# A block-diagonal 128x128 product in a state space layer, written as two products of its 64x64 blocks

## The chip, the cores and the metric

The kernel runs on one core of one Trainium2 chip. The metric is the device time of one execution in microseconds (us). It is given as the median of several executions, beside one execution that the hardware profiler recorded.

## The reference, cut to what matters

The reference is a decoder of four layers over 32 sequences of 64 tokens (2,048 tokens, 256 wide), all in 32-bit floats. Two of its twelve sublayers, `L1_attn` (32 heads) and `L2_attn` (8 heads), are state space mixers. Each head keeps a state that decays by a factor per token:

```python
dt = jax.nn.softplus(dt + dt_bias)
A = -jnp.exp(A_log)
dA = jnp.exp(dt * A)

def step(h, inp):
    dA_t, dt_t, x_t, B_t, C_t = inp
    u = (dt_t[:, :, None] * x_t)[..., None] * B_t[:, :, None, :]
    h = dA_t[:, :, None, None] * h + u
    y = jnp.einsum('bhpn,bhn->bhp', h, C_t)
    return (h, y)
...
y = jnp.moveaxis(ys, 0, 1) + D_param[None, None, :, None] * xs
g = y * _silu(gate)
g = g * jax.lax.rsqrt(jnp.mean(g * g, axis=-1, keepdims=True) + EPS) * norm_w
return jnp.einsum('bli,di->bld', g, W_out)
```

A sequence has 64 tokens and begins with a zero state. So the output of token i is a sum over the tokens s up to i, and the weight of s holds exp of the sum of `dt * A` over the tokens after s up to i. This weight is called the decay here. The kernel makes all decays of a sequence and a head at once, as a 64x64 matrix.

## The kernel before

**Tokens and tiles.** The 2,048 tokens are 16 tiles of 128 partitions, two sequences of 64 in each tile. The state space layers take two tiles at a time (index `t`). `unit_ssm` (L1197) normalises, projects and makes `dt`, `da` (which is `dt * A`) and the masked product of B and C, `cb`. `unit_ssm_heads` (L1229) then does eight heads at a time: four calls for a pair of tiles in `L1_attn`, one call in `L2_attn`. With eight pairs of tiles in each layer that is 32 + 8 = 40 calls.

**The decays.** In each call `ra` (2 tiles, 8 heads, 64 columns) holds `da` of token s in row s, and zero in the columns of earlier tokens. The constant `after` (L53) is 1 where the row is a later token than the column *and both belong to the same sequence*: a 128x128 matrix of two 64x64 blocks on the diagonal and zeros elsewhere. The product of `after` with `ra[:, t]` (L1249, through the helper `prod`, L755) is the sum of `da` over the tokens between, for 8 heads x 64 columns = 512 columns, in one PSUM bank. ScalarE takes `Exp` of it into `m` (L1250), VectorE multiplies by `cb` (L1251), and the 64x64 products of L1273 use it. There are two such products in a call, 80 in the kernel.

**PSUM and TensorE.** Every product writes a tile `mm` of one bank, of which there are eight. A product of 128 rows by 128 columns of weights takes the whole array. One with 64 rows and 64 columns takes a quarter, chosen by the partitions that it reads and writes. Such quarters are used elsewhere already: L1273 (64 columns), and `cross_out` (L1015), where a 64x64 block of the context meets 512 columns. There, and at L1273, the two row halves write into different banks; the two column halves of one row half share a bank.

**The order.** Nothing runs in the order of the Python code. A `Recorder` (L376) collects every operation with its dependencies, and `Order.run` (L562) then places them one after the other: of the operations that are ready, the one that can start first on its engine, by the planner's own durations. Some operations may go to either of two engines (`either`, `combine`), and the planner chooses. The streams of three groups of tiles (8, 6 and 2) are woven together, and a limit (`horizon`, 120 us of TensorE work by the same durations) keeps the planner from running too far ahead. All instructions are issued from one line, L2326, so groups of the profile are told apart by the names of tiles. The durations of TensorE come from these lines:

```python
part = (32 if k <= 32 else 64 if k <= 64 else 128) * (32 if m <= 32 else 64 if m <= 64 else 128) / 16384

if part == 1:
    return max(n, m) * 0.00168 + 0.004
return max(0.068, n * 0.00168 * part * 1.2 + 0.02)
```

For a full product over 512 columns they give 0.864 us, and for a 64x64 one over 512 columns 0.278 us.

In the names of the profile, `pair_mm` are the projections of the state space layers (128 rows, 256 columns), `ssm_heads_mm` all products of `unit_ssm_heads`, and `ssm_heads_mm<-ssm_heads_b,__init___consts` of the shape 128x512 the product with `after`.

Of the kernel before, what the change touches and what calls it, by code (L numbers as in the profile page):

```python
# [199 lines left out]
def bc(ap, axis, n):  # L200

    u = ap.unsqueeze(axis)
    s = list(u.shape)
    s[axis] = n
    return u.broadcast_to(s)
# [11 lines left out]
def split(ap, a, pat="p (a b) -> p a b"):  # L217
    return ap.rearrange(pat, a=a)
# [425 lines left out]
class Net:  # L644
# [584 lines left out]
    def unit_ssm_heads(self, W, nh, g, j, st):  # L1229

        nc = self.nc
        nx = nh // 2
        wx, wg, wr, wo, par = W
        cw = par["cw"].rearrange("p (c k) -> p c k", k=4)
        upto = self.k("upto")
        first, last = j == 0, j + 4 == nx
        hT, dt, da, cb = st["hT"], st["dt"], st["da"], st["cb"]

        ra = self.b4(2, 8, 64)
        nc.combine(  # L1240
            ra, bc(da[:, :, 2 * j : 2 * j + 8], 3, 64), bc(bc(upto, 1, 2), 2, 8), ALU.mult
        )
        xs = self.b4(4, GT)
        for u in range(0, 4, 2):
            self.conv(par, cw, xs[:, u : u + 2, :], self.pair(wx, (j + u) * P, hT), j + u)
        gs, m = self.b4(4, GT), self.b4(2, 8, 64)
        for t in range(2):
            ps = self.mm()
            self.prod(ps, [(self.k("after"), ra[:, t])])  # L1249
            nc.scalar.activation(m[:, t], split(ps, 8), AF.Exp)  # L1250
        nc.vector.tensor_tensor(m, m, bc(cb, 2, 8), ALU.mult)  # L1251
        for u in range(0, 4, 2):
            nc.scalar.activation(gs[:, u : u + 2, :], self.pair(wg, (j + u) * P, hT), AF.Silu)
        xd = self.b4(2, 8, 64)
        for t in range(2):
            ps = split(self.mm(), 4)
            for u in range(4):
                self.transpose(ps[:, u, :], xs[:, u, t * P : (t + 1) * P])
            nc.vector.tensor_tensor(
                xd[:, t],  # L1260
                ps.rearrange("p c (h n) -> p (c h) n", h=2),
                bc(dt[:, t, 2 * j : 2 * j + 8], 2, 64),
                ALU.mult,
            )

        y = self.b4(4, GT)
        pv = [self.mm().rearrange("p (u t n) -> p u t n", u=4, t=2) for b in range(2)]
        for t in range(2):
            for u in range(4):
                for b in range(2):  # L1270
                    rb = slice(64 * b, 64 * b + 64)
                    for h in range(2):
                        nc.tensor.matmul(  # L1273
                            pv[b][64 * h : 64 * h + 64, u, t],
                            xd[rb, t, 2 * u + h, :],
                            m[rb, t, 2 * u + h, :],
                            start=True,
                            stop=True,
                        )
        y5 = y.rearrange("p u (t b n) -> p u t b n", t=2, b=2)  # L1280
        x5 = xs.rearrange("p u (t b n) -> p u t b n", t=2, b=2)
        for b in range(2):
            for u in range(4):
                nc.vector.scalar_tensor_tensor(
                    y5[:, u, :, b], x5[:, u, :, b], par["d"][:, j + u : j + u + 1], pv[b][:, u], ALU.mult, ALU.add
                )
        nc.combine(y, y, gs, ALU.mult)
        sq = self.b4(4, GT)
        nc.scalar.activation(sq, y, AF.Square)


        if first:
            st["acc"] = [self.mm() for _ in range(2)]
        acc = st["acc"]
        pq = acc[0][:, 256:]
        for u in range(4):
            if u == 3:
                for v in range(4):
                    rows = slice(32 * v, 32 * v + 32)
                    nc.tensor.matmul(pq[rows, :], self.k("unit"), sq[:, v, :], start=False, stop=False)  # L1300
            for t in range(2):
                nc.tensor.matmul(
                    acc[t][:, :256],
                    y[:, u, t * P : (t + 1) * P],
                    wo[(j + u) // 8][:, (j + u) % 8, :],
                    start=(first and u == 0),
                    stop=(last and u == 3),
                )
        if not last:
            return  # L1310

        sums = self.tmp(GT)
        self.evac(sums, pq)
        pr = self.mm()
        for t in range(2):
            self.prod(pr[:, t : t + 1], [(sums[:, t * P : (t + 1) * P], self.k("ones")[:, 0:1])])
        ve, rs = self.sm(2), self.sm(2)
        nc.vector.tensor_scalar(ve, pr[:, :2], 1.0 / (nx * P), 1e-5, ALU.mult, ALU.add)
        self.power(rs, ve)
        for t in range(2):  # L1320
            self.outproj(2 * g + t, acc[t][:, :256], rs[:, t : t + 1])
# [1103 lines left out]
```

## Time and profile before

| | |
|---|---|
| median of 9 executions | 3210.51 us (3189.45 to 3213.98) |
| the profiled execution | 3188.77 us |
| its span, first to last instruction | 3186.7 us |
| TensorE (PE) busy | 2978.2 us, 93% of the span |
| VectorE (DVE) busy | 2216.9 us, 70% |
| ScalarE (ACT) and GpSimd (POOL) busy | 1413.5 us and 1412.6 us, 44% each |
| mean granted TensorE clock | 0.969 |

The page gives the busy time of each engine, and groups instructions by tile names and shape. A 32-bit matmul leaves two records in the trace, so the 80 products with `after` are 160 records. The duration of one record includes the time in which the next record already streams. How long a matmul holds TensorE is therefore read from the distance between the starts of two records, not from a duration. "PEld" is the weight load, which runs beside the matmul before it.

### The profile page before, as it was taken

What the parts mean: (1) busy time and instruction counts of PE and PEld (TensorE: products, weight loads), DVE (VectorE), ACT (ScalarE), POOL (GpSimd) and SP (SyncE); (2) the same over time, 40 slices, a digit from 0 to 9 for tenths busy, and PEclk for the clock granted to TensorE, in tenths of its full rate; (3) what the DMA queues carried; (4) which work ended last, traced back from release to release, by engine and by line L of the source; (5) the groups of instructions that cost most, each with busy time, mean ns of one, the idle gap of its engine ahead of it and who ended that gap; (6) DMA issues with size and microseconds to landing.
All of it is one profiled execution on the core that took longest, in us unless ns stands there. A gap on an engine that the chain in (4) does not pass through costs nothing.

```text
span 3186.7 us, 66434 instructions
## 1 busy us (share of the span) xinstructions
PE 2978.2 (93%) x26862; PEld 2369.1 (74%) x26862; DVE 2216.9 (70%) x5239; ACT 1413.5 (44%) x2623; POOL 1412.6 (44%) x1278
## 2 busy tenths in 40 slices
PE   8999999999999899999989999999999988996689
PEld 7888887777777788788767777767787757774467
DVE  5564347775456577755889988777657879786684
ACT  1233325566442233544545555553335654453341
POOL 4442232224454555225653456565634655354230
PEclk9999999999999999999999999999999999997789
DMA  4104120031431533012001010103561120224240
GB/s 154 33 16 171 62 87 10 1 144 57 178 132 43 154 118 117 30 57 70 28 26 31 1 64 8 69 19 125 171 241 62 61 69 15 82 92 142 82 178 27
DMA packets 112949, 256.97 MB, mean 81 GB/s; under 512 B 26309, under 2 KB 73688, under 8 KB 100228
## 3 DMA queue, kind: packets, MB, share of 16 engines
q1 hardware_dynamic: 97860, 204.73, 18.5%
q0 software_dynamic: 14784, 48.01, 4.4%
q8 instruction: 212, 3.47, 0.4%
q14 instruction: 93, 0.76, 0.1%
HBM read 177.34 MB, written 78.77 MB: 80 GB/s over the span
## 4 chain that ended last, share of the span: by engine, by line
PE 65%; DVE 20%; ACT 5%; POOL 5%; issue 3%; DMA 1%; SPq 0%; DVEq 0%; POOLq 0%; ACTq 0%
PE L_xattn_mm L2326 9%; PE L_attn_mm L2326 8%; PE cross_out_mm L2326 8%; PE ssm_heads_mm L2326 7%; PE pair_mm L2326 5%; DVE ssm_heads_b L2326 4%; PE L_ffn_mm L2326 4%; PE turn_mm L2326 4%; PE rope_mm L2326 3%; PE L_block_mm L2326 3%; DVE L_xattn_b L2326 2%; PE L_dense_mm L2326 2%; PE L_experts_mm L2326 2%; PE heads_mm L2326 1%; DVE L_xattn_sm L2326 1%
## 5 line engine op out<-in xcount | busy, mean ns | idle before, releaser
L2326 PE MATMUL pair_mm<-norm_b,load_ssm_w 128*128 128x256 f32 x1280 | 306.9, 385 | 0.9 <-DVE ssm_heads_b L2326 0.6
L2326 PEld LDWEIGHTS pair_mm<-norm_b,load_ssm_w 128*128 128x128 f32 x1280 | 238.4, 192 | 45.5 <-issue 9.1
L2326 DVE SCALAR_TENSOR_TENSOR ssm_heads_b<-pair_mm,load_ssm_wp,ssm_heads_b 128x252 f32<-128x252 f32 (+2 forms) x480 | 218.9, 473 | 17.9 <-ACT ssm_heads_b L2326 8.0
L2326 POOL TENSOR_TENSOR L_xattn_sm<-L_xattn_sm,__init___consts 128x8 f32<-128x8 f32 (+2 forms) x62 | 178.5, 2881 | 86.1 <-DVE L_xattn_sm L2326 77.3
L2326 ACT ACT_TABLE_LOAD x153 | 196.3, 1283 | 32.8 <-PE L_block_mm L2326 11.6
L2326 POOL TENSOR_TENSOR norm_sm<-norm_sm,__init___consts 128x1 f32<-128x1 f32 (+1 forms) x142 | 88.6, 626 | 257.4 <-DVE norm_sm L2326 246.0
L2326 ACT COPY L_xattn_b<-L_xattn_mm 128x512 f32<-128x512 f32 x189 | 110.8, 588 | 188.8 <-PE L_xattn_mm L2326 188.6
L2326 ACT COPY turn_b<-turn_mm 128x512 f32<-128x512 f32 x202 | 112.7, 588 | 179.7 <-PE turn_mm L2326 176.5
L2326 PE MATMUL ssm_heads_mm<-load_ssm_w,ssm_heads_b 128*128 128x256 f32 x640 | 161.2, 396 | 6.7 <-issue 3.7
L2326 PE MATMUL rope_mm<-norm_b,load_L_attn_w 128*128 128x128 f32 x1280 | 160.9, 282 | 3.8 <-DMA load_L_attn_w<-in_a_wk 3.2
L2326 PEld LDWEIGHTS rope_mm<-norm_b,load_L_attn_w 128*128 128x128 f32 x1280 | 152.8, 196 | 9.0 <-issue 6.0
L2326 POOL TENSOR_TENSOR ssm_heads_b<-ssm_heads_b,ssm_heads_b 128x1024 f32<-128x1024 f32 x30 | 70.8, 2360 | 188.6 <-DVE ssm_heads_b L2326 142.5
L2326 PEld LDWEIGHTS ssm_heads_mm<-load_ssm_w,ssm_heads_b 128*128 128x128 f32 x640 | 119.3, 194 | 42.2 <-issue 19.8
L2326 PEld LDWEIGHTS L_xattn_mm<-norm_b,load_L_xattn_w 128*128 128x128 f32 x1024 | 119.3, 192 | 8.3 <-issue 7.0
L2326 ACT ACTIVATE ssm_heads_b<-pair_mm,load_ssm_wp 128x256 f32<-128x256 f32 x160 | 81.6, 560 | 96.8 <-PE pair_mm L2326 94.9
L2326 PE MATMUL L_xattn_mm<-norm_b,units_L_xattn_w 128*128 128x128 f32 x1024 | 122.5, 276 | 2.1 <-ACT norm_b L2326 1.4
L2326 PE MATMUL L_xattn_mm<-norm_b,load_L_xattn_w 128*128 128x128 f32 x1024 | 123.1, 276 | 0.0
L2326 POOL DMA_INDIRECT slots<-norm_b,L_ffn_sm x84 | 91.0, 1083 | 69.4 <-DVE L_ffn_b L2326 22.9
L2326 PEld LDWEIGHTS L_xattn_mm<-norm_b,units_L_xattn_w 128*128 128x128 f32 x1024 | 118.3, 192 | 4.3 <-ACT norm_b L2326 1.8
L2326 DVE TENSOR_TENSOR rope_b<-rope_mm,__init___consts 128x512 f32<-128x512 f32 x160 | 102.7, 680 | 25.3 <-PE rope_mm L2326 14.4
L2326 PE MATMUL L_attn_mm<-load_L_attn_w,L_attn_b 128*128 128x256 f32 x512 | 119.2, 385 | 0.7 <-ACT L_attn_b L2326 0.5
L2326 PE MATMUL cross_out_mm<-units_L_xattn_w,cross_out_b 128*128 128x256 f32 x512 | 116.1, 383 | 3.9 <-ACT cross_out_b L2326 3.9
(437 smaller groups left out, 7740.8 us busy)
## 6 DMA issues: line engine op xcount, KB each, us to landing
queue<-far_w SPq DMA_DIRECT2D x14, 1024.0 KB
L_block_w<-in_f_rows SPq DMA_DIRECT2D x16, 770.0 KB
load_ssm_w<-in_s_in SPq DMA_DIRECT2D x12, 1024.0 KB
parts<-far_w SPq DMA_DIRECT2D x10, 1024.0 KB
slots<-far_w SPq DMA_DIRECT2D x16, 548.0 KB
L_experts_b<-slots SPq DMA_DIRECT2D x32, 274.0 KB
units_L_xattn_w<-kept_x SPq DMA_DIRECT2D x8, 1024.0 KB
L_parts_b<-parts SPq DMA_DIRECT2D x14, 512.0 KB
```

The source lines that it names most:

```text
L2326: done = getattr(getattr(nc, e), method)(*map(real, op.args), **{k: real(v) for k, v in op.kw.items()})
```

## The change

The product over 128 rows becomes two products over 64 rows each, with the two diagonal blocks of the same constant. The first reads partitions 0 to 63 and writes partitions 0 to 63 of the bank, the second does the same with 64 to 127. The blocks left out hold zeros only. `Exp` and everything behind it stay as they are.

```diff
         for t in range(2):
+
             ps = self.mm()
-            self.prod(ps, [(self.k("after"), ra[:, t])])
+            for b in range(2):
+                rb = slice(64 * b, 64 * b + 64)
+                nc.tensor.matmul(ps[rb], self.k("after")[rb, rb], ra[rb, t], start=True, stop=True)
             nc.scalar.activation(m[:, t], split(ps, 8), AF.Exp)
```

The planner reads the new shapes, so its durations for these operations change with them: 0.864 us for the old product, 2 x 0.278 = 0.556 us for the two new ones. The order of the instructions is planned anew from that.

## The prediction

> **What bounds the kernel now.** I read the page's busy times first, then the chain that ended last, then busy times by stretch, and last the order of TensorE's records around a product with `after`.
>
> ```profile
> PE 2978.2 (93%) x26862; PEld 2369.1 (74%) x26862; DVE 2216.9 (70%) x5239; ACT 1413.5 (44%) x2623; POOL 1412.6 (44%) x1278
> PE 65%; DVE 20%; ACT 5%; POOL 5%; issue 3%; DMA 1%; SPq 0%; DVEq 0%; POOLq 0%; ACTq 0%
> ```
>
> The first line is the busy time of the engines, the second the chain's shares by engine. TensorE is busy 93% of the span and carries 65% of the chain: it is the bound, with 3186.7 - 2978.2 = 208.5 us in which it is idle. In the busy times by stretch (us, then PE, PEld, DVE, ACT and POOL busy, granted clock, DMA share, GB/s) I look at where state space heads run alone, and at their last appearance:
>
> ```profile
> 489.00:752.00 263.00, 260.18 (x2241) 201.99 (x2240) 199.59 (x461) 161.85 (x252) 62.42 (x37) 1.00 0.15 56
> 2850.00:2910.00 60.00, 39.46 (x323) 28.45 (x314) 42.87 (x133) 27.70 (x47) 28.24 (x29) 0.82 0.21 65
> ```
>
> From 489 to 752 us TensorE has 2.8 us of idle time in 263: what a product costs there is paid in full. From 2850 to 2910 it is idle for 20.5 of 60 us, at a granted clock of 0.82. Now the groups (busy us, mean ns of one record):
>
> ```profile
> L2326 PE MATMUL ssm_heads_mm<-ssm_heads_b,__init___consts 128*128 128x512 f32 x160 | 79.1, 612 | 2.0 <-DVE ssm_heads_b L2326 1.0 <-POOL ssm_heads_b L2326 0.9
> L2326 PE MATMUL cross_out_mm<-turn_b,context_cx 64*64 64x512 f32 x512 | 74.6, 645 | 0.5 <-ACT turn_b L2326 0.5
> ```
>
> The first is what the change replaces: 80 matmuls, 79.1 us. The second is the nearest relative of what replaces it: 256 matmuls with 64x64 weights over 512 columns, 74.6 / 256 = 0.29 us each. Taken alone, that row promises 160 x 0.29 = 46.6 us for the new products, a gain of 32 us, and the planner's own 0.278 us says the same. The timeline (start, length, records) shows why I don't take it.
>
> ```profile
> 500.25 1.88 PE L2326 MATMUL ssm_heads_mm<-ssm_heads_b,__init___consts 128*128 128x512 f32 x4
> 501.97 0.59 PE L2326 MATMUL pair_mm<-norm_b,load_ssm_w 128*128 128x256 f32 x2
> ...
> 1310.53 0.59 PE L2326 MATMUL pair_mm<-norm_b,load_ssm_w 128*128 128x256 f32 x2
> 1311.05 1.08 PE L2326 MATMUL cross_out_mm<-turn_b,context_cx 64*64 64x512 f32 x4
> 1312.06 0.55 PE L2326 MATMUL ssm_heads_mm<-__init___consts,ssm_heads_b 128*128 128x128 f32 x3
> ...
> 2053.96 1.93 PE L2326 MATMUL cross_out_mm<-turn_b,context_cx 64*64 64x512 f32 x12
> 2055.83 0.48 PE L2326 MATMUL cross_out_mm<-load_L_xattn_w,cross_out_b 128*128 128x256 f32 x1
> ```
>
> At 500.25 two products with `after` (four records) hold TensorE until 501.97: 1.72 us, 0.86 each. At 1311.05 just two 64x64 matmuls over 512 columns stand between full ones: they hold it until 1312.06, 1.01 us. So two quarters side by side are not faster than one full product. The 0.29 us of the group come from four quarters working at once; each of them still streams its 512 columns for 0.86 us.
>
> **The change, part by part.** *The stream.* Each product uses only two of the four quarters, and the two blocks use them together: 0.86 us for a pair where 0.86 us stood before. At 2053.96 six quarter matmuls, four at once and then two, hold TensorE for 1.87 us, 2 x 0.86 + 0.15, so a second pair behind a first costs 0.86 again. Removed: 80 x 0.86 = 69 us. Added: 80 x 0.86 = 69 us. Nothing is won.
>
> *The change of shape.* The pair at 1311.05 pays 1.01 - 0.86 = 0.15 us for its first fill and for leaving the quarters. It also pays on entry: two `pair_mm` records at 1310.53 should hold TensorE for 2 x 0.216 (306.9 us / 1280 is 0.24 with gaps; start to start it is 0.216), until 1310.96, and the next record starts at 1311.05: 0.09 us. In the records the 0.15 is 0.05 of fill and 0.09 of leaving. The Trainium skill, in TensorEngine Tiling (Array Packing), section Tiling Modes, says that changing the tiling mode drains the TensorE; it gives no price, so the row has it.
>
> How often is this paid? The planned order of both kernels tells it. Among TensorE's matmuls the shape changes 1167 times before and 1223 times after. With the products with `after` on one side, 13 before, 86 after; elsewhere 17 fewer. The new products stand in 48 runs: 31 of four (both tiles of a call), 10 of two, and a few odd ones. So: 73 changes x 0.09 = 6.6 us, 48 first fills x 0.05 = 2.4 us, 17 fewer elsewhere x 0.09 = -1.5 us.
>
> *Halves torn apart.* Six runs are of one or three products. There a half stands without its partner and streams 0.86 us alone, three pairs' worth: 3 x 0.86 = 2.6 us.
>
> *Weights.* 64x64 loads (135 ns a record, from the group of the 64x64 heads) replace 128x128 ones (190 ns). Both lie under a matmul's 430 ns and cost nothing; without that cover it would be 320 x 0.135 = 43 us.
>
> *The rest.* No DMA, buffer or wait is added; ScalarE's `Exp` waits for the second half instead of the one product. Sum: 6.6 + 2.4 - 1.5 + 2.6 = **10.1 us**, on an engine that is busy 93% of the time. I count it in full, since the dense stretches hold most of the 80.
>
> *The order.* The planner believes that each pair is 0.31 us cheaper, 24.6 us in all, and plans anew: TensorE's order is the same for its first 2282 matmuls, then it differs; ScalarE gets 2641 instructions instead of 2625, VectorE 5202 instead of 5209, the function tables load 154 times instead of 153. On engines with 56% and 30% idle time these counts cost nothing by themselves (16 copies of 0.59 us would be 9.4 us if ScalarE bound). What the order does to TensorE's waits no row can tell. I bound it by rows. Below: the 20.5 us of idle time from 2850 to 2910 closes up, and its 39.5 us of work run at the full clock (39.5 x 0.18 = 7 us): -27.5 us. Above: the four longest waits of TensorE in the list of waits, 17.4, 17.0, 16.1 and 10.6 us, grow by half: +31 us. A value near the middle is nearest to the rest of the trace; I take 0, and keep both ends.
>
> *Same bank.* One thing the trace does not show: two row halves writing into one bank at once; L1015 and L1273 give them two banks. If they run together, the pair costs 0.86 us, as above. If they take turns, it costs 1.72 and the kernel 80 x 0.86 = 69 us more. The first is nearer, since the two halves write different partitions, as the two column halves of one row half do at 1311.05, in one bank, side by side. A rule speaks against it: the same page of the Trainium skill, section Restrictions and Gotchas, says that different row tiles cannot access the same PSUM bank simultaneously. By the rule the sum would be +79 us, by the row +10.
>
> **The sum against the time.** The profiled execution took 3188.77 us (2.1 us outside its span), at the low end of the nine, whose median is 3210.5. The sum gives 3198.9 for such an execution, and for the median 3210.5 + 10.1 = 3220.6; I say **3221**.
>
> **Rivals.** No change is what this kernel's measurement can't tell apart: within 0.3%, 9.6 us. All times below are against the median.
>
> 1. *The quarters' price lands on idle time.* If the waits of the woven stretches absorb what is added outside 489 to 752, only the share of the 16 calls there is left: 10.1 x 16/40 = 4 us, 3215. For it: 208.5 us of idle time. Against it: the chain is 65% TensorE.
> 2. *The new order closes the late stretch* (faster). One place, 2850 to 2910, with up to 27.5 us to win: 3210.5 + 10.1 - 27.5 = 3193. It decides once it wins over 10.1 + 9.6 = 19.7 us. For it: the planner works with 24.6 us less on TensorE and can pull work ahead. Against it: it really has 10 us more, so what it pulls ahead comes too early for TensorE.
> 3. *The new order lengthens waits:* 3221 + 31 = 3252. For it: the planner now misjudges 80 places by 0.3 to 0.5 us. Against it: the dense stretch has no waits to lengthen.
> 4. *The halves take turns:* 3210.5 + 10.1 + 69 = 3290.
> That the change is not what it says can be left out: the order shows 160 matmuls of 64x512 in place of 80 of 128x512.
>
> **The numbers.** The forecast (3211 to 3231) gets 0.46, rival 1 0.08, rival 2 0.26, rival 3 0.14, rival 4 0.06. The forecast stands just above the bound of 9.6 us; with a few us of new waits it is over it, so I count 0.38 of it as slower and 0.08 as the same. Slower: 0.38 + 0.14 + 0.06 = 0.58. Same: 0.08 + 0.08 = 0.16. Faster: 0.26. The range reaches from rival 2 to rival 3, 3193 to 3252; rival 4 and the tails of 2 and 3, some 2 in 10, are left out. The forecast's own range is 3211 to 3231.
>
> **What would show it.** In the profile after, the group `ssm_heads_mm` of 64x512 should have 320 records and a busy time of 75 to 90 us (taking turns: about 140). The timeline should show a run of four products held for about 1.87 us, entry 0.09 us late. From 489 on, the first state space stage should take about 0.24 us x 16 = 4 us longer. TensorE's busy time should grow by about 10 us. A gain of TensorE's busy time in that stage would prove the stream's reckoning wrong; a total below 3201 with the pairs as said would prove that the order outweighs them.

## The result and the profile after

The changed kernel takes 3223.83 us (median of 10 executions, 3214.68 to 3231.36). The kernel before, measured beside it and earlier, takes 3206.94 us (median of 31). The ratio is 1.006, with a 95% interval of 1.0041 to 1.008: slower by 13 to 26 us. The forecast was 3221, the range 3193 to 3252. It stood on the median of nine executions, 3210.5; against the later median the change is 16.9 us, where 10.1 were forecast.

The busy times and the shares of the chain by engine in the page after:

```profile
PE 3003.3 (93%) x27022; PEld 2368.2 (74%) x27022; DVE 2220.7 (69%) x5232; ACT 1423.5 (44%) x2639; POOL 1409.4 (44%) x1270
PE 71%; DVE 16%; ACT 4%; POOL 4%; issue 3%; DMA 2%; SPq 0%; DVEq 0%; POOLq 0%; ACTq 0%
```

TensorE is still the bound. Its busy time grew by 25.1 us, more than the sum of 10.1 us. The clock records of the two traces say why: they hold only two levels, 1.0 and 0.5, and TensorE was busy at 0.5 for 151.6 us before and 183.3 us after. Half of that difference, 15.9 us, is time lost to the clock; 9.2 us are left, near the 10.1 (three pages with the work of before scatter by 4 us in this figure). The weight loads are what they were, 2368 us, although there are 160 more records. The group of the product (busy us, mean ns of a record):

```profile
L2329 PE MATMUL ssm_heads_mm<-ssm_heads_b,__init___consts 64*64 64x512 f32 x320 | 83.6, 616 | 2.8 <-DVE ssm_heads_b L2329 2.0 <-POOL ssm_heads_b L2329 0.7
```

It was 79.1 us with 160 records. The timeline shows a run of two pairs (start, length, records):

```profile
499.63 1.03 PE L2329 MATMUL pair_mm<-norm_b,load_ssm_w 128*128 128x256 f32 x4
500.59 1.93 PE L2329 MATMUL ssm_heads_mm<-ssm_heads_b,__init___consts 64*64 64x512 f32 x8
502.45 0.70 PE L2329 MATMUL pair_mm<-norm_b,load_ssm_w 128*128 128x256 f32 x2
```

The four `pair_mm` records should hold TensorE until 499.63 + 4 x 0.216 = 500.49. The next record starts at 500.59: 0.10 us late, the price of entry. The two pairs hold it for 1.86 us, where two full products held it for 1.72. The next full-array record then comes 0.32 us behind the one at 502.45 instead of 0.216: another 0.10 us of leaving, which the prediction did not count. In single records the starts within this run are 0, 7, 480, 487, 909, 916, 1339 and 1345 ns: the two halves of a pair start 7 ns apart and each streams for 430 ns a record. So they work side by side, in one bank.

Two stretches (us, then PE, PEld, DVE, ACT, POOL busy, granted clock):

```profile
489.00:752.00 263.00, 260.69 (x2289) 195.87 (x2289) 198.79 (x459) 159.85 (x247) 59.35 (x35) 0.99 0.15 55
2850.00:2910.00 60.00, 51.31 (x435) 37.52 (x434) 39.58 (x98) 34.59 (x61) 22.20 (x22) 0.83 0.16 48
```

The dense stretch stays full. The idle time from 2850 to 2910, which rival 2 wanted to close, is down from 20.5 to 8.7 us at the same place on the clock, but the work there is another: the span did not get shorter. (With the order of before, other executions below have 11 and 13 us of idle time in the same stretch.)

**The two pages are not at one clock.** The page before was taken at a mean granted clock of 0.969, the page after at 0.964. Every execution of the sets below has its time and its clock on record. Within one kernel they go together: a line fitted through 33 executions of the kernel before and 46 of four variants on one chip, with one slope for all, falls by 2.66 us for each 0.001 of the clock, and single executions lie about 2.6 us off it. So of the 29.8 us between the two spans (3186.7 and 3216.5) some 13 us belong to the clocks of the two executions. Below, "at equal clock" means the distance between two kernels on such a line, with its 95% interval; the ratio is the plain comparison. Each set has its own line, with 2.66, 2.57 and 2.25 us per 0.001.

The clock is not only a matter of the chip. In the traces a stretch at 0.5 lasts 3.4 us or a multiple of it, and mostly follows idle time of TensorE, as here in the trace before (stretches as above, then DMA share, GB/s):

```profile
1041.76:1045.18 3.42, 0.93 (x14) 0.74 (x13) 3.18 (x12) 0.00 (x0) 0.97 (x2) 1.00 0.86 254
1045.18:1052.00 6.82, 6.82 (x54) 6.36 (x53) 3.85 (x6) 0.74 (x2) 5.31 (x6) 0.50 0.20 55
```

In the fourteen traces TensorE was idle for more than a tenth of the 3.4 us before 473 of 494 such stretches, and in only 12% of the windows of 3.4 us that no such stretch followed. So an order that moves idle time may well change the clock, and "at equal clock" takes that part of its price out. The plain ratio keeps it in.

### The profile page after: what moved, and what is told of

It is laid out like the page before. It is cut to its first block, busy times and chain, and to the rows that moved or that the text cites. A ratio compares the mean times of both kernels' runs of the same rounds, so it can differ in the third digit from the quotient of the medians.

```text
span 3216.5 us, 66798 instructions
## 1 busy us (share of the span) xinstructions
PE 3003.3 (93%) x27022; PEld 2368.2 (74%) x27022; DVE 2220.7 (69%) x5232; ACT 1423.5 (44%) x2639; POOL 1409.4 (44%) x1270
## 4 chain that ended last, share of the span: by engine, by line
PE 71%; DVE 16%; ACT 4%; POOL 4%; issue 3%; DMA 2%; SPq 0%; DVEq 0%; POOLq 0%; ACTq 0%
PE ssm_heads_mm L2329 10%; PE L_xattn_mm L2329 9%; PE cross_out_mm L2329 8%; PE pair_mm L2329 8%; PE L_attn_mm L2329 8%; PE L_ffn_mm L2329 4%; PE turn_mm L2329 4%; PE L_block_mm L2329 4%; PE rope_mm L2329 3%; DVE L_xattn_b L2329 2%; PE L_dense_mm L2329 2%; PE heads_mm L2329 2%; DVE L_xattn_sm L2329 1%; PE small_scores_mm L2329 1%; DVE weigh_sm L2329 1%
```

## The experiments

Three sets of four kernels ran, each beside the kernel before. The first set ran on one chip, where the kernel before has a median of 3200.26 us; the other two ran on another chip, where it has 3332.95 and 3333.94 us. Each ratio is against the kernel before in the same set.

### The halves in the old order

```diff
@@ in issue(), with the planner as before
+            if method == "matmul" and op.args[1].t.tag == "consts" and (op.args[1].n, op.args[1].size(), op.args[2].size()) == (128, 128, 512):
+                ps, lhsT, rhs = op.args
+                for r in (slice(0, 64), slice(64, 128)):
+                    nc.tensor.matmul(real(ps[r]), real(lhsT[r, r]), real(rhs[r]), start=True, stop=True)
+                continue
```

> The order is planned with the old product and its old price, and each product is then issued as its two 64x64 halves, side by side, in exactly the place that the product had. TensorE's shape changes 1238 times instead of 1167, no half is torn from its partner, and the products stand in 45 runs. Theory 1 (the change costs its shape changes and fills, the new order the rest): 71 x 0.09 + 45 x 0.05 = 8.7 us slower than before, TensorE's busy time 5 to 9 us longer. Theory 2 (the new order costs nearly all of it): within 3 us of before. Theory 3 (the pairs cost all of it, in waits that the records do not price): 16 to 19 us slower.

Measured: 3208.05 us against 3200.26, ratio 1.0012 (0.9992 to 1.0033). At equal clock the difference is 8.0 us (6.3 to 9.7). The plain ratio alone would not settle it: its interval reaches from 3 us faster to 11 us slower, because these executions had a mean clock of 0.9649 against 0.9638. With the clock taken out, theory 1's 8.7 us lies inside the interval, and theories 2 and 3 lie outside; so does the 4 us of the prediction's rival 1. The group:

```profile
L2329 PE MATMUL ssm_heads_mm<-ssm_heads_b,__init___consts 64*64 64x512 f32 x320 | 80.1, 613 | 1.8 <-DVE ssm_heads_b L2331 1.0 <-POOL ssm_heads_b L2331 0.7
```

80.1 us against 79.1: the streams cost what they did.

Where the rest stands can be read place by place, since both traces hold the same other records in the same order. At each place of the products I took the time from the start of the last record before it to the start of the fifth other record after it. At the 40 of 41 places without a stretch at half clock the halves lengthen it by 9.0 us in all; the column halves of the experiment after next, which keep the shape, by 0.15 us at 39. At 23 of the 40 it is 0.30 to 0.35 us (once 0.64), more than the prediction's 0.24; at 12 it is 0.11 or less. That the sum came to the forecast is in part luck: the full price was too low, and it was counted where it is not paid.

In the dense stage the first and last record of `ssm_heads_mm` are 254.4 us apart before and 256.5 here, so 2.1 us for 16 calls, where the prediction had about 4. In the changed kernel they are 257.2 apart, 6.3 us more than with the whole product in the same order (250.9, next experiment), with a stretch of 3.4 us at half clock among them.

### The whole product in the new order

```diff
@@ in issue(), with the planner and the recorded halves as in the changed kernel
+            if method == "matmul" and op.args[1].t.tag == "consts" and (op.args[1].n, op.args[1].size(), op.args[2].size()) == (64, 64, 512):
+                ps, lhsT, rhs = op.args
+                if ps.p0:
+                    ...
+                    nc.tensor.matmul(*map(real, full), start=True, stop=True)
+                continue
```

> The order is planned with the two halves and their price of 0.556 us, exactly as in the changed kernel, and at the place of the second half the one full product is issued in place of both. TensorE's shape changes 1156 times, against 1167 before. Theory 1: the order's share alone, 5 to 10 us slower than before. Theory 2: 15 to 19 us slower. Theory 3: within 3 us of before.

Measured: 3211.70 us, ratio 1.0031 (1.0012 to 1.005), so 4 to 16 us slower with the work of before. At equal clock it is 6.4 us (4.7 to 8.1), and its executions had a mean clock of 0.9618 against 0.9638, which is worth another 0.002 x 2660 = 5 us; whether that clock belongs to the order or to these twelve executions is not settled. Theory 3 falls: the order has a price of its own. Theory 2's 15 to 19 us for the order alone are above it at equal clock, and at the end of the plain interval. Against the page before, two waits of TensorE stand out (waits in total, times, longest; before, then here):

```profile
PE L_block_mm L2326 <- DVE L_block_b L2326: 7.0, 7, 1.9
PE turn_mm L2326 <- DVE L_xattn_b L2326: 4.2, 3, 3.0
PE L_block_mm L2336 <- DVE L_block_b L2336: 12.6, 8, 4.5
PE turn_mm L2336 <- DVE L_xattn_b L2336: 10.0, 5, 4.1
```

Others went down, `turn_mm` on `L_xattn_b` of POOL from 16.1 to 11.7. In the changed kernel the same two are 11.8 and 10.6 us; in the two runs of this set with the old order they are at most 7.9 and 4.6. These are stages without any state space work: the order moved waits to places that the diff does not touch. It did not add to them: TensorE's idle time in all is 209.9 us here and 207.1 to 210.1 in the three pages with the old order. What is longer in this page is the time busy at half clock, 219.4 us against 151.6 to 193.0, in an execution at the low end of its kernel's clocks. Where the 6.4 us at equal clock stand is open.

### More matmuls without a change of shape

```diff
@@ in issue(), with the planner as before
+                for v in range(2):
+                    nc.tensor.matmul(
+                        real(ps[:, 256 * v : 256 * v + 256]), real(lhsT), real(rhs[:, 4 * v : 4 * v + 4]), start=True, stop=True
+                    )
...
```

> The order is that of before; each product is issued as two full-shape matmuls, of 128x128 weights over 256 columns each, instead of one over 512. It adds the same 80 matmuls and weight loads as the change but no change of shape. Theory 1: no difference, within 3 us of before, since two streams of 256 columns hold TensorE as long as one of 512 and the loads lie under them. Rival (80 more instructions cost by themselves, about 0.1 us each): 8 us slower.

Measured: 3200.79 us, ratio 0.9992 (0.9968 to 1.0015); at equal clock 0.3 us (-1.4 to 2.0). The same 80 additional matmuls and weight loads cost nothing when the shape stays. So the 8 us of the halves are not the price of more instructions.

### All four quarters at once

```diff
+        pa = [self.mm() for _ in range(2)]
         for t in range(2):
-            ps = self.mm()
-            self.prod(ps, [(self.k("after"), ra[:, t])])
-            nc.scalar.activation(m[:, t], split(ps, 8), AF.Exp)
+            for b in range(2):
+                rb, ro = slice(64 * b, 64 * b + 64), slice(64 * (b ^ t), 64 * (b ^ t) + 64)
+                nc.tensor.matmul(pa[t][ro], self.k("after")[rb, rb], ra[rb, t], start=True, stop=True)
+        for t in range(2):
+            nc.scalar.activation(m[:, t], split(pa[t], 8), AF.Exp)
@@ in unit_ssm: dt a third time, in swapped rows of the second tile
+        for b in range(2):
+            at = slice(P + 64 * (1 - b), P + 64 * (1 - b) + 64)
+            self.prod(pd[64 * b : 64 * b + 64, 2, :], [(hT[:, c, at], wr[:, c, 256:]) for c in range(2)])
...
-        nc.vector.tensor_tensor(da, dt, bc(par["alog"], 1, 2), ALU.mult)
+        nc.vector.tensor_tensor(da, dt[:, ::2], bc(par["alog"], 1, 2), ALU.mult)
```

> Both products of a call fill all four quarters: for the second tile the two sequences stand in swapped rows of the factor (its dt is made a second time in swapped rows by four small matmuls in each of the 16 pairs of tiles), so its halves use the two quarters that the first tile leaves free. The planner's price of four halves is 1.11 us. By the records four quarters at once hold TensorE for 0.86 us plus 0.24 for the change of shape, where two full products held it for 1.72: 40 x 0.62 = 25 us less; the small matmuls, a change of shape of 0.18 us and about 0.3 us of issue in each of 16 places, take back 8. Theory 1: 17 us faster than before, with 10 us to either side for the new order. Rival (halves that write the same bank from different rows gain nothing over one after the other): no faster than before, 10 to 20 us slower.

Measured: 3218.19 us, ratio 1.0047 (1.0024 to 1.0069). The expectation of 17 us faster is missed. The mechanism itself works, as a run of four halves in the timeline and the group show:

```profile
498.51 1.09 PE L2333 MATMUL ssm_heads_mm<-ssm_heads_b,__init___consts 64*64 64x512 f32 x8
499.53 0.92 PE L2333 MATMUL pair_mm<-norm_b,load_ssm_w 128*128 128x256 f32 x3
```

```profile
L2333 PE MATMUL ssm_heads_mm<-ssm_heads_b,__init___consts 64*64 64x512 f32 x320 | 51.4, 612 | 1.8 <-DVE ssm_heads_b L2333 0.9 <-POOL ssm_heads_b L2333 0.7
```

Eight records hold TensorE for 1.02 us instead of 1.72, and the group takes 51.4 us instead of 79.1. So the rival's reason, halves that gain nothing in one bank, is wrong although its sign was right. Of the 27.7 us saved, the small matmuls that make `dt` a third time take back 7.0 us (two groups of 3.7 and 3.3). The rest did not reach the end. At equal clock the kernel stands where the kernel before does (-0.7 us, interval -3.0 to 1.6), and its mean clock is 0.9577 against 0.9638, which is worth 16 us. Its ten executions lie at 0.955 to 0.961, those of before at 0.960 to 0.969, so the lower clock belongs to this kernel. The stretches show both (here, here, and the second one before):

```profile
489.00:752.00 263.00, 254.76 (x2326) 193.81 (x2325) 210.72 (x462) 160.96 (x251) 57.11 (x34) 0.99 0.15 55
1880.00:2380.00 500.00, 466.22 (x4348) 365.57 (x4347) 348.56 (x866) 240.33 (x475) 270.60 (x245) 0.94 0.28 96
1880.00:2380.00 500.00, 470.67 (x4421) 371.55 (x4420) 366.18 (x908) 234.68 (x463) 284.73 (x258) 0.97 0.29 99
```

In the dense stage TensorE is now idle for 8.2 us where it was 2.8. From 1880 to 2380, far from any of the removed work, the clock is 0.94 against 0.97 before; but the page with the halves in the old order has 0.95 there, so the execution makes a good part of that difference. Which idle time brought this kernel's clock down was not tried further.

### Is it the planner's price, or any new order?

Four kernels change only what the planner is told. The first keeps the four quarters, the second the changed kernel's halves, the others the kernel before.

```diff
         k, m, n = lhsT.n, lhsT.size(), rhs.size()
+        if lhsT.t.tag == "consts" and (k, m, n) == (64, 64, 512):
+            return 0.432
```

> Four quarters as in the run before, but the planner is told 0.432 us for each half, 1.73 us for the four, as the two full products cost it. The work of TensorE is that of the four quarters, the order another. Theory 1 (what the quarters save is real, and the order that went with it gave it back in waits and clock): the order decides, so the time is anywhere between 17 us faster than before and 15 us slower, and compared at the same mean granted clock it is not slower than before. Rival (the saved time is not on the path in any order): the same time as in the run with four quarters, 15 to 18 us slower than before, with the same lower clock of 0.957 to 0.958.

> The changed kernel, with the planner told 0.432 us for each half, so that a pair costs it 0.864 us as the full product did. The order follows that of before for the first 6169 matmuls and then differs. TensorE's shape changes 1250 times against 1167, two halves' worth of pairs are torn. Theory 1 (price of the pairs, and an order that is a matter of chance): 83 x 0.09 + 47 x 0.05 + 2 x 0.86 = 11.5 us slower, with 10 us to either side for the order. Theory 2 (the order's share came from the planner's too low price): 9 to 12 us slower and no more, since the price is now right.

```diff
         k, m, n = lhsT.n, lhsT.size(), rhs.size()
+        if lhsT.t.tag == "consts" and (k, m, n) == (128, 128, 512):
+            return 0.840        # 0.900 in the other
```

> The kernel before, with nothing changed but the planner's price of the full product: 0.840 us instead of 0.864. The work is the same and the price is off by 3%. Theory 1 (any new order moves the time by several us, whatever the price): a difference from before of 3 to 15 us, of either sign. Theory 2 (a price that is nearly right plans nearly as well): within 3 us of before.

> The kernel before, with the planner's price of the full product at 0.900 us instead of 0.864. Theory 1: a difference from before of 3 to 15 us, of either sign. Theory 2: within 3 us of before.

| planner's price | median, us | ratio to before (95%) | at equal clock, us | mean clock (before 0.945) |
|---|---|---|---|---|
| quarters, 0.432 a half | 3370.99 | 1.0124 (1.0093 to 1.0155) | 24.1 | 0.9388 |
| halves, 0.432 each | 3373.35 | 1.0129 (1.0098 to 1.016) | 25.6 | 0.9388 |
| product, 0.840 | 3329.88 | 1.0004 (0.9985 to 1.0022) | -0.8 | 0.9450 |
| product, 0.900 | 3316.65 | 0.9951 (0.9931 to 0.9971) | -17.5 | 0.9437 |

The quarters at the old price missed both of their expectations: they are 38 us slower by the medians, and at equal clock not level but 24.1 us slower. The halves at a fair price are 41 us slower by the means, more than twice what the changed kernel costs with its too low price. So theory 2, that the order's share comes from the planner's error about the halves, falls. Theory 1's margin of 10 us was too narrow as well. With the work of before untouched, a price 4% off makes it 16 us faster by the medians, and 3% off the other way gives nothing: neither theory names both. An order has a time of its own, and how near a price is to the truth does not tell it. Counted in matmul records done, both slow kernels fall behind the product at 0.840 on the same chip mostly between 1880 and 2380 us; the second of them, and that product:

```profile
1880.00:2380.00 500.00, 449.74 (x3926) 345.58 (x3924) 321.79 (x792) 212.98 (x428) 243.45 (x208) 0.87 0.15 51
```

```profile
1880.00:2380.00 500.00, 460.96 (x4139) 352.01 (x4138) 345.56 (x843) 227.84 (x452) 277.54 (x242) 0.92 0.20 67
```

In the same 500 us the slow kernel gets 213 matmul records less done, at a clock of 0.87 instead of 0.92, with 50 us of TensorE idle instead of 39.

### The changed kernel, the better order, and the halves in it

The changed kernel and the product at 0.900 ran once more, unchanged. The third kernel issues the halves in the order of the 0.900 price, with the edit of the first experiment, and the fourth is the four quarters at a price of 0.240 a half.

> The changed kernel once more, on the chip of this set, beside the kernel before and the next two. Theory 1 (its parts add up: 8 us for the pairs in the old order, 2.6 us for halves torn apart, 7 to 10 us for the new order): 17 to 21 us slower than before. Rival (the order's share is a matter of one chip): the pairs' share remains, 8 to 11 us, and the order's share may have any value from -15 to 30 us.

> The kernel before with the planner's price of the product at 0.900 us, once more. Theory 1 (an order has its own time, most of which it keeps from chip to chip): 8 to 20 us faster than before. Rival (the gain belonged to that chip): within 8 us of before, of either sign.

> The order of the run with the price of 0.900 us, place by place, with each product issued as its two halves side by side. Against that run, TensorE's shape changes 1223 times instead of 1150, in 46 runs of products, and no half is torn off. Theory 1 (the pairs have one price in any order): 73 x 0.09 + 46 x 0.05 = 8.9 us slower than the run with the whole product in this order. Rival (the price of 8 us belonged to the old order): within 3 us of it, or more than 14 us slower.

> Four quarters at once, with the planner told 0.240 us for each half, 0.96 us for the four. The work is that of the first run with four quarters, the order another. Theory 1 (the quarters save 17 us of TensorE's time, and the order decides what is left of it): between 25 us faster and 15 us slower than before. Rival (the saving is never on the path): 12 us slower or more, as in both runs with four quarters so far.

| kernel | median, us | ratio to before (95%) | at equal clock, us (95%) |
|---|---|---|---|
| the changed kernel | 3345.52 | 1.0031 (1.0016 to 1.0047) | 10.3 (8.2 to 12.4) |
| product, planner's price 0.900 | 3316.15 | 0.9942 (0.9921 to 0.9962) | -14.7 (-17.4 to -12.0) |
| halves in that order | 3316.49 | 0.9944 (0.9926 to 0.9963) | -11.3 (-13.7 to -8.9) |
| quarters, 0.240 a half | 3328.29 | 0.9980 (0.9962 to 0.9998) | -7.6 (-9.7 to -5.5) |

The changed kernel is slower on this chip too, by 5 to 16 us, less than the 17 to 21 of the parts' sum. If the halves and torn pairs take 8 to 11 us here as well, little is left for the order, as the rival had it: the order's share would then depend on the chip. The whole product in the new order was not run on this chip, and the intervals of the first result and of this one, 13 to 26 and 5 to 16 us, overlap.

The gain of the 0.900 order came again on the same chip, 0.6%; it is the version that beats both kernels, with the whole product. Whether it keeps the gain on the other chip was not run.

The halves in that order missed theory 1's 8.9 us: 0.3 us by the medians, 3.4 us at equal clock with some 3 us to either side. So less arrives at the end than in the old order, by intervals that just overlap (0.2 to 6.5 here, 6.3 to 9.7 there). At their places they cost the same. Read as in the first experiment, against the run with the whole product in this order, the places grow by 8.7 us in all, at 40 of 43 without a stretch at half clock. So TensorE pays theory 1's price in this order too, and some 5 us of it do not arrive at the end. That later idle time takes them up, as the prediction's rival 1 had it, is not shown: TensorE's idle time is 277.9 us in this page and 273.8 in the other.

The quarters in a third order are 0.2% faster than before, after two orders in which they were 0.5% and 1.2% slower. The rival's forecast of 12 us or more is missed. That the quarters' saving is what arrived is not shown: the 0.900 order alone gained more, without any saving.

## Why the prediction was right

- **The stream: right.** Two quarters side by side hold TensorE as long as one full product (1.86 us for two pairs with their change of shape, forecast 1.87). The row of 0.29 us for four quarters would have promised a gain of 32 us; the run with four quarters shows that it needs all four (1.02 us for both products).
- **The change of shape: right in its sum, not in its price.** Entry 0.10 us against 0.09. In the old order the halves cost 9.0 us at their places and 8.0 us (6.3 to 9.7) at the end at equal clock, where the same terms gave 8.7. The full price of one place is 0.35 us, not 0.24, and it is not paid at all of them. In another order they cost 8.7 us at their places, and 3.4 us were left at the end; what took up the rest is open.
- **More instructions and weight loads at nothing: right**, by the run with column halves (0.3 us) and by the unchanged weight load time.
- **Same bank: the halves run side by side**, 7 ns apart. The rule of the Trainium skill in TensorEngine Tiling (Array Packing), section Restrictions and Gotchas, that different row tiles cannot access the same PSUM bank simultaneously, is not borne out for halves that write different partitions of it. Rival 4 falls with it.
- **Torn halves, 2.6 us: too high.** Against the whole product in the same order, the places in the changed kernel grow by 9.8 us in all (42 of 45 without a stretch at half clock), torn halves included, where 6.6 + 2.4 + 2.6 = 11.6 was counted. Only two places grow by more than 0.5 us, 0.72 and 0.82, both with a torn pair: less 0.35 each, that is an estimate of 0.8 us for the torn halves.
- **The order: the term that was mis-sized.** It was taken as 0 between -27.5 and +31 us. With the whole product in the new order it is 6.4 us at equal clock and 12 us by the means on the first chip. Rival 3, longer waits, is not what the pages show: the waits on `L_block_b` and `L_xattn_b` grew, but the idle time in all did not. By which way the order cost its 6 to 12 us stays open; a lower clock may be part of it.
- **Rival 2** did not come for this change. The 0.900 price gained 15 to 18 us at equal clock by the order alone, less than rival 2's 27.5; that it came from the late stretch is not shown.

The 17 us between the medians are then about 10 for the halves, torn ones included, and about 6 for the order at equal clock. That the parts come from another set than the first result, whose chip is not on record, and that the second chip gives 12 us in all, limits this sum. The forecast of 3221 against 3223.83 is nearer than its working deserves, and that is luck: the difference was 16.9 us and not 10.1, the order, taken at 0, made up most of the 6.8 between them, and the median of nine that the sum was added to was 3.6 us above the later one.

## What to carry to other kernels

A matmul on a quarter of the array streamed its 512 columns here for as long as one on the whole (0.86 us); the gain came only with all four quarters at work, so ask how many are filled, not how small the tile is. Read the price of a small matmul from a place where it stands as it will stand, not from a group's mean. Where two kernels issue the same instructions in the same order, compare their traces place by place: that gave 9.0 us against a control of 0.15, where the medians could not tell. Where a planner orders the instructions, run the new work in the old order and the old work in the new order before crediting or blaming the change: here one changed price of the planner, with no change to the work, moved the kernel before by up to 0.6%, and the changed kernel from 0.3% to 1.3% slower on the same chip.

## What the runs showed of the hardware that was not expected

The mean granted clock differs from execution to execution of one kernel (0.960 to 0.969 for the kernel before on the first chip), and the time goes with it, 2.66 us per 0.001. That is 24 us between the ends, more than the change itself. Comparing pages at different clocks as if they were one hides effects of this size; a line through all executions brought the standard deviation down from 7.6 us (the kernel before alone) to about 2.6 us.

The kernel before took 3333 us on one chip and 3200 on another, at mean clocks of 0.945 and 0.964. By the slope of the clock that is 50 of the 133 us. The two pages of the changed kernel, with spans of 3216.5 and 3350.0 us, are as far apart. In them TensorE is idle for 213.2 and 269.9 us, 57 more, and busy at half clock for 183.3 and 313.4 us, which loses another 65. Why there is more idle time on the second chip was not looked into.
